# A graph kernel: where five pieces of work stand in the round of jobs, and which engine adds a bias

## The chip, the cores and the metric

The kernel runs on one core of a Trainium2 chip. A core has a matrix engine (TensorE, PE in the profile, with its weight loads shown as PEld), a vector engine (VectorE, DVE), an activation engine (ScalarE, ACT), a general engine (GpSimd, POOL) and a queue engine that only issues DMAs here (SyncE, SP). Matmuls write to PSUM, a small memory that VectorE and ScalarE read and write too. The metric is the device time of one execution in microseconds (us), lower is better.

## What is computed

There are 128 graphs with 128 nodes and 64 features each. Layer 0 normalises the features, takes the relu, and sums a message over all pairs of neighbours; layer 1 normalises again and multiplies with the weighted adjacency.

```python
h = max(layernorm(x), 0)
mask = adj > 0
A = h @ W1[:64] + h @ W1[64:] + b1          # per node j
C = h @ W1[64:]                             # per node k
hm[j] = sum over k of mask[j, k] * relu(A[j] - C[k])     # 192 hidden units
x = x + hm @ W2 + (number of neighbours of j) * b2
h = max(layernorm(x), 0)
x = x + (adj @ h) @ W.T
```

(Written here with the difference in the message multiplied out, as the kernel does it.) About one pair in eight is an edge, so the kernel doesn't compute all pairs: it gives every node j a fixed number of slots for its neighbours and gathers the neighbours' rows by matmuls with one-hot matrices.

## The kernel before, in words

**Groups.** The graphs are done in 32 groups of four (`G = 4`, `NG = 32`). A group's work has three parts: what is prepared in the round of the group ahead, the main jobs, and what is finished in the round of the group behind. In a node's neighbour list the 128 nodes k are cut into four quarters of 32 (`Q`, `QN`), and each node has six slots (`D`) in each quarter. The few neighbours beyond are handled by `edge_x`, `edge_sum` and `edge_sum1`, with the one-hot matrices `R`, `RT` and `S2`.

**Preparation** (table `AHEAD`, for group g + 1 in the round of group g):

- `pre_adj` transposes adj on TensorE (`pt`), copies it (`adjT`) and makes the mask (`maskT`, on VectorE; two buffers, so it waits until `edge_sum` of the group before last has read its own). It also starts the norm's statistics (`sta`, `mva`).
- `pre_norm` and `pre_hT` make the normalised features `h` and their transpose `hT`.
- `pre_rank` counts with one matmul (`pq`) which slot each neighbour takes; ScalarE copies the ranks to `qs`, VectorE marks the overflow (`ov`).
- `pre_slots`, in three pieces, compares the ranks with the slot numbers on VectorE and makes the one-hot matrix `S`. After the last piece twelve DMAs on SyncE's queue copy it into `S3`, in which the quarters stand three times below each other.
- `pre_count` (`pd`) counts neighbours and makes the small per-node factors `dn`, `ns`, `half`, `nb`.
- `pre_proj`, for r = 0 and r = 1, is the projection, of two graphs each: four fp32 matmul passes give C, A and the output row (`pp`, in one of the three large PSUM tiles `g`), and two bf16 matmuls add the biases to the columns from H on (`oneb` times `biasp`, a split of the fp32 bias into three bf16 parts in three rows). ScalarE copies the result to bf16 (`ca`, first part), makes `z` and `e` from it, VectorE subtracts the copy from the fp32 value (`rest`), ScalarE rounds that (second part), GpSimd the remainder (third part). So three bf16 parts stand for the fp32 value.
- `pre_stack`: twelve DMAs on SyncE's queue put the parts of `ca` into `k3`, by part and quarter.
- `pre_edge_a` to `pre_edge_d` and `pre_place` make the one-hot matrices of the overflowing edges.

**Jobs.** A round has 24 jobs (`Job`, times t = 0 to 23, list `ORDER`). A job fills one of three PSUM tiles `g`, each two banks, by matmuls of `k3` with `S3` and with an identity (`id3`), and drains it. A job of kind 0 has the first 128 hidden units of one graph; VectorE drains it with one reduction (`hm`). A job of kind 1 has the last 64 units of two graphs, one on each half of the columns; ScalarE takes the relu (`T`) and GpSimd sums. In a round four jobs of kind 0 are followed by two of kind 1, four times over, so t = 4, 5, 10, 11, 16, 17, 22, 23 are of kind 1. The jobs at t = 0 and 1 need the last of the twelve `k3` copies.

**Finishing** (table `BEHIND`, for group g − 1): `slot_sum` adds two halves on GpSimd; `edge_sum` (24 matmuls `pe`) and `edge_sum1` (ten) correct the sums and VectorE makes `u0` (128 units) and `u1` (64 units of two graphs); `post0` multiplies by W2 (`py`; `w2bd` takes `u1` over all columns, `w2h` takes `u0` on one half of the columns for each pair); `post1` transposes back (`pty`), adds `e` and computes the second norm's statistics; `post2` makes the second `h`; `post3` multiplies by the adjacency (`pga`, on halves of the columns); `post4` by W, adds, and stores.

**Order.** All matmuls run in the order in which the program writes them (`mm` and `tp` call `keep_in_program_order`): per t first the job's matmuls, then the pieces of `OWN`, `BEHIND` and `AHEAD` of that t. On the other engines and on SyncE's queue the written order is kept in the start only (`Engine.held`). In the rounds the framework's planner orders each queue when the program is built: of the instructions it believes to be ready it takes the one written first. That order is then fixed. The last group has its own list (`ORDERL`), and its finishing pieces run alone at the end.

Of the kernel before, what the change touches and what calls it, by code (L numbers as in the profile page):

```python
# [8 lines left out]
F32 = mybir.dt.float32  # L9
BF16 = mybir.dt.bfloat16  # L10
I32 = mybir.dt.int32
AF = mybir.ActivationFunctionType
ALU = mybir.AluOpType
# [137 lines left out]
def kernel(  # L151
# [28 lines left out]
    def mm(*args, **kw):  # L180
        return tc.keep_in_program_order(nc.tensor.matmul(*args, **kw))  # L181
# [21 lines left out]
    vec, act, pool, sp = (Engine(e) for e in (nc.vector, nc.scalar, nc.gpsimd, nc.sync))  # L203

    B, N, F = x.shape
    H = W1.shape[1]
    O = W2.shape[1]
    P = 128
# [19 lines left out]
    with ExitStack() as main:  # L228
        const = main.enter_context(tc.tile_pool(name="const", bufs=1))
        loads = main.enter_context(tc.tile_pool(name="loads", bufs=2))  # L230
        grp = main.enter_context(tc.tile_pool(name="grp", bufs=2))
        one = main.enter_context(tc.tile_pool(name="one", bufs=1))
# [4 lines left out]
        def gtile(name):  # L237
            return ps_g.tile([P, 2, 512], F32, tag="g", name=name)
# [10 lines left out]
        w2bd = const.tile([P, 2, O], F32, tag="w2bd", name="w2bd")  # L249
# [3 lines left out]
        ident = const.tile([P, P], F32, tag="ident", name="ident")  # L253
        make_identity(nc, ident)

        id64 = const.tile([P, 4], F32, tag="id64", name="id64")
        vec.tensor_tensor(id64, ident[:, 0:4], ident[:, F : F + 4], ALU.add)
        ones = const.tile([P, P], F32, tag="ones", name="ones")
        pool.memset(ones, 1.0)
        oneb = const.tile([P, P], BF16, tag="oneb", name="oneb")  # L260
# [11 lines left out]
        for q in range(Q):  # L272
            s = slice(q * QN, (q + 1) * QN)
# [43 lines left out]
        bias = const.tile([P, H + O], F32, tag="bias", name="bias")  # L317
        wp = const.tile([P, 2 * H + O], F32, tag="wp", name="wp")
        wab = wp[:, H : 2 * H]
        biasp = const.tile([P, H + O], BF16, tag="biasp", name="biasp")  # L320

        def weight_loads():
            act.dma_start(w2a, W2[0:C0, :])
# [33 lines left out]
            return pc  # L357

        def weights_c(pc):
            left = bias  # L360
            for i in range(3):
                pt = one.tile([P, H + O], BF16, tag=f"bp{i}", name=f"bp{i}")
                vec.tensor_copy(pt, left)

                if i == 0:
                    vec.tensor_scalar(biasp, pt, id64[:, i : i + 1], None, ALU.mult)
                    vec.tensor_copy(wp[:, 2 * H : 2 * H + O], pc[:, 0:O])
                else:
                    vec.scalar_tensor_tensor(
                        biasp, pt, id64[:, i : i + 1], biasp, ALU.mult, ALU.add  # L370
                    )
                if i < 2:
                    nxt = one.tile([P, H + O], F32, tag=f"br{i}", name=f"br{i}")
                    vec.tensor_tensor(nxt, left, pt, ALU.subtract)
                    left = nxt

        def weights_d():
            pl = mtile("pl")
# [5 lines left out]
        def bc(t, n, axis):  # L384
            shape = list(t.shape)
            shape.insert(axis, n)
            return t.unsqueeze(axis).to_broadcast(shape)
# [150 lines left out]
        def pre_proj(g, r):  # L538

            d = groups[g]  # L540
            if r == 0:

                d["ca"] = grp.tile([P, 3, 2, G, H], BF16, tag="ca", name=f"ca{g}")

                d["z"] = grp.tile([P, G, C0], F32, tag="z", name=f"z{g}")
                d["z1"] = grp.tile([P, 2, 2, C1], F32, tag="z1", name=f"z1{g}")
                d["e"] = grp.tile([P, G, O], F32, tag="e", name=f"e{g}", bufs=3)
            pp = gtile(f"pp{g}_{r}")
            for p in range(2):
                s = slice(p * F, (p + 1) * F)  # L550
                mm(
                    pp[:, p, 0 : 2 * H + O], d["hT"][s, r], wp[s, :],
                    start=True, stop=False, skip_group_check=True,
                )
            for p in range(2):
                s = slice(p * F, (p + 1) * F)
                mm(
                    pp[:, p, H : 2 * H + O], oneb[s, :], biasp[s, :],
                    start=False, stop=True, skip_group_check=True,
                )  # L560
            x = pp[:, :, 0 : 2 * H].rearrange("n p (t u) -> n p t u", t=2)
            parts = [
                d["ca"][:, i].rearrange("n t (p r) u -> n r p t u", p=2)[:, r] for i in range(3)
            ]
            act.activation(parts[0], x, AF.Copy)
            rest = tmp.tile([P, 2, 2, H], F32, tag="rest", name=f"rest{g}_{r}")

            def zs():
                for p in range(2):
                    b = 2 * p + r  # L570
                    for to, us, f in (
                        (d["z"][:, b], slice(0, C0), AF.Abs),
                        (d["z1"][:, r, p], slice(C0, H), AF.Relu),
                    ):
                        act.activation(to, x[:, p, 1, us], f, scale=d["ns"][:, b : b + 1])


            def es():
                for p in range(2):
                    b = 2 * p + r  # L580
                    act.activation(
                        d["e"][:, b], pp[:, p, 2 * H : 2 * H + O], AF.Copy,
                        scale=d["dn"][:, 0, b : b + 1],
                    )

            def second():
                act.activation(parts[1], rest, AF.Copy)

            def third(engine):
                for t in range(2):  # L590
                    engine.tensor_tensor(
                        parts[2][:, :, t], rest[:, :, t], parts[1][:, :, t], ALU.subtract
                    )

            def add_x():
                pool.tensor_tensor(d["e"], d["e"], d["x"], ALU.add)

            if g == 0:
                vec.tensor_tensor(rest, x, parts[0], ALU.subtract)
                return zs, es, second, third, add_x  # L600
            zs()
            es()
            vec.tensor_tensor(rest, x, parts[0], ALU.subtract)
            second()
            third(pool)
            if r == 1:
                add_x()
# [143 lines left out]
        def post0(g):  # L751
            d = groups[g]
            py = mtile(f"py{g}")
            d["py"] = py
            for p in range(2):
                s = slice(p * O, (p + 1) * O)
                mm(
                    py[s, 0 : 2 * N], w2h,
                    d["u0"][:, 2 * p : 2 * p + 2].rearrange("h r j -> h (r j)"),
                    start=True, stop=False, skip_group_check=True,  # L760
                )
            w = w2bd.rearrange("h p o -> h (p o)")
            mm(
                py[:, 0 : 2 * N], w, d["u1"].rearrange("h r j -> h (r j)"),
                start=False, stop=True, skip_group_check=True,
            )
            d["ys"] = tmp.tile([P, 2, N], F32, tag="ys", name=f"ys{g}", bufs=1)
            act.activation(
                d["ys"].rearrange("p r j -> p (r j)"), py[:, 0 : 2 * N], AF.Copy
            )  # L770
# [47 lines left out]
        class Job:  # L818
# [70 lines left out]

        AHEAD = {  # L890
            0: (pre_adj,),
            2: (pre_norm, pre_hT,),
            3: (pre_rank, lambda g: pre_slots(g, 0, 2),),
            4: (lambda g: pre_slots(g, 2, 4),),
            5: (pre_count,),
            6: (lambda g: pre_slots(g, 4, D),),
            7: (lambda g: pre_proj(g, 0),),
            9: (pre_edge_a,),
            12: (lambda g: pre_proj(g, 1), pre_stack,),
            19: (pre_edge_b,),  # L900
            20: (pre_place,),
# [7 lines left out]
        BEHIND = {  # L909
            0: (slot_sum,),  # L910
            1: (edge_sum,),
            4: (edge_sum1,),
            8: (post0,),
            10: (post1,),
            15: (post2,),
            16: (post3,),
            19: (post4,),
        }

# [33 lines left out]
        pc = weights_b()  # L953
# [80 lines left out]
```

## Time and profile before

| | us |
|---|---|
| median of three executions | 994.23 (993.23 to 1002.85) |
| the profiled execution | 1005.13 |
| its span, first to last instruction | 1003.4 |
| TensorE, VectorE, ScalarE, GpSimd busy | 947.9, 801.2, 706.3, 767.5 |
| SyncE waiting for a VectorE result before the `S` copies, in total | 256.3 in 29 times |
| one `S` copy, issue to landing, median | 4.0 |
| one `k` copy, issue to landing, median | 2.2 |

The page's busy time of TensorE counts matmuls that overlap in its pipeline and stretches in which one waits inside, so a high share does not say that it works at its best rate. A few of the costliest groups of instructions, as line, engine, operation, output<-inputs, shapes and count | busy us, mean ns of one | idle time before them and what ended it:

```profile
L198 DVE TENSOR_REDUCE hm<-g 128x64 f32<-128x768 f32 x512 | 473.4, 950 | 117.0 <-PE g L181 113.2
L181 PE MATMUL pp<-wp,hT 64*128 64x448 f32 x256 | 68.5, 613 | 0.0
L198 ACT ACTIVATE ca<-pp 128x768 bf16<-128x768 f32 x64 | 51.4, 804 | 63.7 <-PE pp L181 63.7
L198 DVE TENSOR_TENSOR rest<-pp,ca 128x768 f32<-128x768 f32 x64 | 60.7, 949 | 3.0 <-ACT ca L198 2.8
```

The line numbers are those of helpers: L181 and L184 are `mm` and `tp`, L198 is `Engine`, which passes on every call to the other engines. So instructions are told apart by the tiles that they write and read. Times in the timelines are the start from the span's beginning and the duration. "SPq" is SyncE's queue.

### The profile page before, as it was taken

The page shows a single profiled execution, that of the slowest core. Times are in us where ns is not written, and L with a number is a line of the kernel's source. Part 1 is how long each engine was busy: PE and PEld are TensorE (multiplying, and loading weights), DVE is VectorE, ACT ScalarE, POOL GpSimd, SP SyncE. Part 2 cuts the span into 40 slices and gives each one's busy share as a digit, 9 for nine tenths or more (in the row PEclk, how much of TensorE's full clock was granted, in tenths as well). Part 3 has the DMA queues.
Part 4 walks back from the last instruction along what each step waited for, and adds up shares of the span by engine and source line. Part 5 has one row for each costly group of instructions (what it writes and reads, how often), then busy time and mean ns, then how long its engine had stood idle before and what let it go on. Part 6 is the DMA issues. An engine that isn't in the chain of part 4 may idle for free.

```text
span 1003.4 us, 26630 instructions
## 1 busy us (share of the span) xinstructions
PE 947.9 (94%) x9994; PEld 695.8 (69%) x9994; DVE 801.2 (80%) x1769; ACT 706.3 (70%) x1732; POOL 767.5 (76%) x1134
## 2 busy tenths in 40 slices
PE   3899999999999999999999999999999999999996
PEld 2577776677776777777677767677767777777674
DVE  7677888877888878788887787887888887788863
ACT  5557876667877767787677785677787677787652
POOL 3287877787877878877788786778877788787783
PEclk9599999999999999999999999999999999999997
DMA  3626665556766555766555765555766655665520
GB/s 87 134 69 160 153 139 131 127 121 150 157 138 139 129 122 136 164 143 142 126 125 126 159 148 123 124 126 136 164 141 138 134 127 124 157 148 127 111 60 13
DMA packets 88293, 129.89 MB, mean 129 GB/s; under 512 B 47200, under 2 KB 63968, under 8 KB 88160
## 3 DMA queue, kind: packets, MB, share of 16 engines
q1 hardware_dynamic: 87584, 127.98, 56.4%
q8 instruction: 80, 1.31, 0.5%
q14 instruction: 53, 0.43, 0.1%
q10 hardware_dynamic: 576, 0.16, 0.1%
HBM read 13.01 MB, written 4.19 MB: 17 GB/s over the span
## 4 chain that ended last, share of the span: by engine, by line
PE 37%; DVE 23%; ACT 19%; DMA 7%; POOL 6%; issue 4%; SPq 3%; DVEq 0%; POOLq 0%; ACTq 0%
PE g L181 21%; DVE hm L198 7%; DVE S L198 7%; PE pe L181 7%; DMA k<-ca 6%; ACT ca L198 5%; ACT et L198 4%; POOL T L198 4%; SPq L198 3%; ACT h L198 3%; ACT T L198 3%; DVE u L198 3%; POOL ca L198 2%; ACT z L198 2%; PE px L181 2%
## 5 line engine op out<-in xcount | busy, mean ns | idle before, releaser
L198 POOL TENSOR_TENSOR T<-T 128x192 f32<-128x192 f32 (+2 forms) x768 | 545.7, 717 | 124.3 <-ACT T L198 84.4
L198 DVE TENSOR_REDUCE hm<-g 128x64 f32<-128x768 f32 x512 | 473.4, 950 | 117.0 <-PE g L181 113.2
L181 PEld LDWEIGHTS <-k 96*128 96x128 bf16 (+1 forms) x6144 | 412.8, 104 | 213.9 <-issue 87.0
L181 PE MATMUL g<-S,k 96*128 96x384 bf16 (+1 forms) x2048 | 392.5, 333 | 34.9 <-DMA k<-ca 18.5
L181 PE MATMUL g<-id,k 96*128 96x192 bf16 (+1 forms) x4096 | 383.9, 248 | 0.0
L198 ACT ACTIVATE T<-g 128x768 f32<-128x768 f32 x256 | 210.2, 823 | 51.7 <-PE g L181 45.7
L198 POOL TENSOR_TENSOR ca<-rest,ca 128x384 bf16<-128x384 f32 x126 | 113.9, 924 | 85.3 <-ACT ca L198 83.6
L198 ACT ACTIVATE ca<-pp 128x768 bf16<-128x768 f32 x64 | 51.4, 804 | 63.7 <-PE pp L181 63.7
L198 DVE TENSOR_TENSOR S<-qs,rks 128x1024 bf16<-128x1024 bf16 x93 | 86.8, 934 | 0.0
L198 ACT ACTIVATE hT<-ph 128x256 f32<-128x256 f32 x32 | 12.3, 384 | 89.4 <-PE ph L184 89.4
L181 PE MATMUL pe<-RT,X 128*64 128x128 f32 (+1 forms) x512 | 71.3, 282 | 0.0
L181 PE MATMUL pp<-wp,hT 64*128 64x448 f32 x256 | 68.5, 613 | 0.0
L198 ACT ACTIVATE z<-pp,ns 128x128 f32<-128x128 f32 (+1 forms) x256 | 66.0, 348 | 0.0
L198 DVE TENSOR_TENSOR rest<-pp,ca 128x768 f32<-128x768 f32 x64 | 60.7, 949 | 3.0 <-ACT ca L198 2.8
L198 ACT ACTIVATE ca<-rest 128x768 bf16<-128x768 f32 x64 | 55.2, 862 | 9.3 <-DVE rest L198 9.2
L181 PEld LDWEIGHTS pe<-RT,X 128*64 128x64 f32 (+1 forms) x512 | 53.4, 166 | 5.3 <-issue 5.3
L198 ACT ACTIVATE et<-et,half 128x128 f32<-128x128 f32 x128 | 56.8, 449 | 0.0
L181 PE MATMUL px<-ca,S 128*128 128x192 bf16 x384 | 52.7, 246 | 0.0
L181 PE MATMUL px<-ca,R 128*128 128x192 bf16 x384 | 52.6, 246 | 0.0
L198 ACT ACTIVATE h<-x,mrb,rsb 128x64 f32<-128x64 f32 x128 | 51.6, 479 | 0.8 <-DVE mrb L198 0.8
L181 PE MATMUL pe<-ident,z 128*128 128x128 f32 x192 | 49.9, 287 | 0.0
L198 ACT ACTIVATE h<-x,mra,rsa 128x64 f32<-128x64 f32 x128 | 48.7, 432 | 1.1 <-DVE mra L198 1.1
(128 smaller groups left out, 1203.9 us busy)
## 6 DMA issues: line engine op xcount, KB each, us to landing
S<-S SPq DMA_DIRECT2D x372, 192.0 KB, 4.0
k<-ca SPq DMA_DIRECT2D x384, 96.0 KB, 2.2
adj<-in_adj_dram SPq DMA_DIRECT2D x32, 256.0 KB, 3.1
x<-in_x_dram SPq DMA_DIRECT2D x32, 128.0 KB, 2.7
out_dram<-ot SPq DMA_DIRECT2D x32, 128.0 KB, 2.2
w<-in_L_gnn_W_dram SPq DMA_DIRECT2D x2, 96.0 KB, 4.4
bias<-in_L_gnn_b_dram ACTq DMA_DIRECT2D x1, 96.0 KB, 3.8
w2a<-in_L_gnn_W_dram ACTq DMA_DIRECT2D x1, 32.0 KB, 2.1
```

Source lines behind the costliest of these rows:

```text
L181: return tc.keep_in_program_order(nc.tensor.matmul(*args, **kw))
L198: ins = f(*args, **kw)
```

## The change

Three things change.

1. **The bias.** The two bias matmuls of each projection go, with `biasp` and what made it at the start (`id64` and the loop in `weights_c`). In their place VectorE adds the fp32 bias to columns H to 2H + O of both banks of the PSUM tile, in place, in one instruction of 128 x 512 elements. The copy `ca`, `z`, `e` and `rest` read the tile after that.
2. **The order inside `post0`.** The matmul with `w2bd`, on all columns, comes first, and the two with `w2h`, on a half of the columns each, come last.
3. **The tables.** `pre_rank` moves from t = 3 to 2, `pre_edge_a` from 9 to 8, `edge_sum1` from 4 to 3, `post0` from 8 to 9, `post1` from 10 to 13, `post2` from 15 to 14, `post3` from 16 to 17. So `edge_sum1` and `post0`, which end with matmuls on halves of the columns, stand right before two jobs of kind 1, and `post3` right behind two of them.

```diff
         def weights_c(pc):
-            left = bias
-            for i in range(3):
-                pt = one.tile([P, H + O], BF16, tag=f"bp{i}", name=f"bp{i}")
-                vec.tensor_copy(pt, left)
...
+            vec.tensor_copy(wp[:, 2 * H : 2 * H + O], pc[:, 0:O])
...
                 mm(
                     pp[:, p, 0 : 2 * H + O], d["hT"][s, r], wp[s, :],
-                    start=True, stop=False, skip_group_check=True,
-                )
-            for p in range(2):
-                s = slice(p * F, (p + 1) * F)
-                mm(
-                    pp[:, p, H : 2 * H + O], oneb[s, :], biasp[s, :],
-                    start=False, stop=True, skip_group_check=True,
-                )
+                    start=True, stop=True, skip_group_check=True,
+                )
+            biased = pp[:, :, H : 2 * H + O]
+            vec.tensor_tensor(biased, biased, bc(bias, 2, 1), ALU.add)
...
             d["py"] = py
-            for p in range(2):
-                s = slice(p * O, (p + 1) * O)
-                mm(
-                    py[s, 0 : 2 * N], w2h,
-                    d["u0"][:, 2 * p : 2 * p + 2].rearrange("h r j -> h (r j)"),
-                    start=True, stop=False, skip_group_check=True,
-                )
             w = w2bd.rearrange("h p o -> h (p o)")
             mm(
                 py[:, 0 : 2 * N], w, d["u1"].rearrange("h r j -> h (r j)"),
-                start=False, stop=True, skip_group_check=True,
-            )
+                start=True, stop=False, skip_group_check=True,
+            )
+            for p in range(2):
+                s = slice(p * O, (p + 1) * O)
+                mm(
+                    py[s, 0 : 2 * N], w2h,
+                    d["u0"][:, 2 * p : 2 * p + 2].rearrange("h r j -> h (r j)"),
+                    start=False, stop=True, skip_group_check=True,
+                )
...
         AHEAD = {
             0: (pre_adj,),
-            2: (pre_norm, pre_hT,),
-            3: (pre_rank, lambda g: pre_slots(g, 0, 2),),
+            2: (pre_norm, pre_hT, pre_rank),
+            3: (lambda g: pre_slots(g, 0, 2),),
             4: (lambda g: pre_slots(g, 2, 4),),
             5: (pre_count,),
             6: (lambda g: pre_slots(g, 4, D),),
             7: (lambda g: pre_proj(g, 0),),
-            9: (pre_edge_a,),
+            8: (pre_edge_a,),
...
         BEHIND = {
             0: (slot_sum,),
             1: (edge_sum,),
-            4: (edge_sum1,),
-            8: (post0,),
-            10: (post1,),
-            15: (post2,),
-            16: (post3,),
+            3: (edge_sum1,),
+            9: (post0,),
+            13: (post1,),
+            14: (post2,),
+            17: (post3,),
             19: (post4,),
         }
```

More of the change, by code (lines that the diff above doesn't have):

```diff
@@ L254 @@
         make_identity(nc, ident)
-        id64 = const.tile([P, 4], F32, tag="id64", name="id64")
-        vec.tensor_tensor(id64, ident[:, 0:4], ident[:, F : F + 4], ALU.add)
         ones = const.tile([P, P], F32, tag="ones", name="ones")
@@ L319 @@
         wab = wp[:, H : 2 * H]
-        biasp = const.tile([P, H + O], BF16, tag="biasp", name="biasp")
         def weight_loads():
@@ L359, in weights_c @@
         def weights_c(pc):
-            left = bias
-            for i in range(3):
-                pt = one.tile([P, H + O], BF16, tag=f"bp{i}", name=f"bp{i}")
-                vec.tensor_copy(pt, left)
[L365 to L370, printed above, removed]
-                    )
[L372 to L375, printed above, removed]
+            vec.tensor_copy(wp[:, 2 * H : 2 * H + O], pc[:, 0:O])
         def weights_d():
@@ L754, in post0 @@
             d["py"] = py
+            w = w2bd.rearrange("h p o -> h (p o)")
+            mm(
+                py[:, 0 : 2 * N], w, d["u1"].rearrange("h r j -> h (r j)"),
+                start=True, stop=False, skip_group_check=True,
+            )
             for p in range(2):
@@ L759, in post0 @@
                     d["u0"][:, 2 * p : 2 * p + 2].rearrange("h r j -> h (r j)"),
-                    start=True, stop=False, skip_group_check=True,
+                    start=False, stop=True, skip_group_check=True,
                 )
-            w = w2bd.rearrange("h p o -> h (p o)")
-            mm(
-                py[:, 0 : 2 * N], w, d["u1"].rearrange("h r j -> h (r j)"),
-                start=False, stop=True, skip_group_check=True,
-            )
             d["ys"] = tmp.tile([P, 2, N], F32, tag="ys", name=f"ys{g}", bufs=1)
```

## The prediction

> **What bounds the kernel now.** I read the busy shares first, then the waits, then one steady group on the SyncE, VectorE, ScalarE and TensorE timelines. The shares would say TensorE:
>
> ```profile
> PE 947.9 (94%) x9994; PEld 695.8 (69%) x9994; DVE 801.2 (80%) x1769; ACT 706.3 (70%) x1732; POOL 767.5 (76%) x1134
> ```
>
> But the waits say that TensorE is stopped by the DMAs that bring `k3` in:
>
> ```profile
> PE g L181 <- DMA k<-ca: 18.5, 22, 7.2
> PEld L181 <- DMA k<-ca: 15.5, 29, 2.4
> ```
>
> (Total, times, longest.) The 7.2 is the start; after it TensorE or its weight loads, which can wait for the same copy, are stopped in nearly every group. So something else closes the loop. Follow one group. VectorE first:
>
> ```profile
> 335.53 0.78 DVE L198 TENSOR_SCALAR maskT<-adjT 128x512 bf16<-128x512 f32 x1 [1.14 <-PE pe L181]
> 336.83 1.81 DVE L198 TENSOR_REDUCE hm<-g 128x64 f32<-128x768 f32 x2
> 340.84 1.00 DVE L198 TENSOR_TENSOR S<-qs,rks 128x1024 bf16<-128x1024 bf16 x1
> 341.97 2.81 DVE L198 TENSOR_REDUCE hm<-g 128x64 f32<-128x768 f32 x3
> 344.70 0.95 DVE L198 TENSOR_TENSOR rest<-pp,ca 128x768 f32<-128x768 f32 x1
> ```
>
> SyncE's queue and then TensorE:
>
> ```profile
> 341.87 10.16 SPq L198 DMA_DIRECT2D S<-S  x12
> 352.12 9.30 SPq L198 DMA_DIRECT2D k<-ca  x12
> ```
> ```profile
> 361.14 0.32 PE L181 MATMUL g<-S,k 96*128 96x384 bf16 x1
> 361.79 0.34 PE L181 MATMUL g<-S,k 96*128 96x384 bf16 x1 [0.32 <-DMA k<-ca]
> 362.73 0.68 PE L181 MATMUL g<-S,k 96*128 96x384 bf16 x2
> ```
>
> The loop: `maskT` starts at 335.53; VectorE works without a gap until the last `S` piece is done at 341.84 (6.3 us); SyncE issues twelve `S` copies (to 352.03) and twelve `k` copies without a gap (to 361.42, 19.6 us together); the last `k` lands 2.2 us after its issue, near 363.0; TensorE then finishes the job at t = 1 and the 24 matmuls of `edge_sum` (2.03 us), and the next `maskT` starts at 365.87. That is 30.3 us. TensorE's spare time is read from the same rows: a job takes 0.66 us (355.33 to 355.99); the job at t = 0 took from 361.14 to 362.29, the one at t = 1 from 362.73 to 363.58, so 0.49 + 0.19 = 0.7 us of waiting. In the chain, `edge_sum` starts at 95.46 and at 963.06, 29 groups apart: 29.9 us a group. A group is as long as this loop, and a change moves the time if it moves a term of the loop, or uses up the slack of what must be ready beside it. The slacks: TensorE's 0.7 us; and the second part of `ca`, which the fifth `k` copy needs.
>
> **The change, part by part, per group.**
>
> *Bias matmuls away (2 pairs).* The second pair starts at 349.15, the next job at 349.41: at most 0.26 us a pair. The least is its 256 columns at the rate of the id matmuls (four of 192 columns in 0.33): 0.11. TensorE saves 0.2 to 0.5.
>
> *Moved matmuls.* A job's four id matmuls take 0.33 us; where a piece with other rows or columns follows, a gap opens: 343.29 + 0.33 = 343.62, and `py` starts at 343.71. Such gaps are 0.09 to 0.16 each. `edge_sum1`, `post0` and `post1` now stand so that about five fewer occur: 0.5 us. [...] Together TensorE gets 0.7 to 1.0 us shorter, inside a slack, so by itself worth 0.
>
> *`pre_rank` from 3 to 2, `edge_sum1` from 4 to 3.* Between `maskT` and the last `S` piece VectorE has no gap, and the same instructions must still be done before it (two `hm`, `u` twice, `ov`, three `S`). Earlier ranks change their order, not their sum: 0. It would be one `hm` (0.87) either way, if the planner put a reduction behind or ahead of the last `S`; I keep both for the range.
>
> *The added VectorE instruction.* 128x512 fp32, read from PSUM and written there. No row writes PSUM from VectorE; with a PSUM source, 256 columns take 0.41, 512 take 0.676 (`u<-hs,pe`), 768 take 0.949 (`rest`). I take 0.68, between 0.41 and 0.95. Two a group: 1.4 us on an engine that had 2.4 idle behind t = 15 and none between 335.5 and 346.
>
> *What it puts in line.* The first copy `ca` of r = 0 ran at once, in ScalarE's idle time, while VectorE was late:
>
> ```profile
> 342.45 0.81 ACT L198 ACTIVATE ca<-pp 128x768 bf16<-128x768 f32 x1 [1.87 <-PE pp L181]
> 344.06 0.55 ACT L198 ACTIVATE e<-pp,dn 128x64 f32<-128x64 f32 x2
> 345.68 0.84 ACT L198 ACTIVATE ca<-rest 128x768 bf16<-128x768 f32 x1 [0.26 <-DVE rest L198]
> 349.61 0.80 ACT L198 ACTIVATE ca<-pp 128x768 bf16<-128x768 f32 x1
> 353.33 0.89 ACT L198 ACTIVATE ca<-rest 128x768 bf16<-128x768 f32 x1
> ```
>
> Now it waits for the add, and the add waits behind the reductions of t = 6 and 7, which are written before it and are ready: 341.97 + 2 × 0.87 + 0.68 = 344.4. So `ca` starts 2.0 us later. Queued behind it on ScalarE: `z`, `e`, the second copy, `ys`, `et`, and the copies of t = 10 and 11; ScalarE has no longer gap from 345.7 to 354. `rest` starts after `e` ends (344.61, then 344.70), so the projection's PSUM tile, one of three, is held to 347.6 and not 345.65. [...]
>
> *r = 1.* The tile for it is free between 348.4 (as before) and 349.6 (if only the reduction of t = 12 frees one); four matmuls take 0.85, so they end at 349.3 to 350.5 (before, with the bias pair, 349.4). The add goes behind that reduction: 349.6 to 350.6. From `ca` to the end of the second part is 4.6 us in the rows (349.61 to 354.22), with the add and a hand-over 5.3 less the 0.4 that ScalarE spent on other work: 354.5 to 355.5. The fifth `k` copy is due at 352.12 + 4 × 0.775 = 355.2. So this slack, 1.0 now, goes to between 0.7 and −0.3.
>
> *`post1` 10 to 13, `post2` 15 to 14, `post3` 16 to 17.* From `pty` (346.39) to the last `h` (353.49) is 7.1 us now; bare, the pieces sum to 3.9 (0.44 + 0.42 + 0.60 + 0.36 + 0.29 + 0.35 + 1.4). Behind `pty` TensorE now has four jobs (2.8) and two `px` (2.0) before `pga`: 4.7. So the wait at `pga` is 0 (bare) to 2.4 (with as much queueing as now); I take 0.3, near the bare sum because `post2` now stands directly behind. From the end of the projection to `pga` it is five jobs (3.4), `pty` 0.37 and the two `px`: 5.8. TensorE reaches t = 18 at 349.9 (middle) + 5.8 + 0.3 + 0.44 = 356.4, against 355.33 before: 1.1 late, its own savings already in it. Less the slack of 0.7: **+0.4 us a group**. Bounds: an early tile and no wait, 349.3 + 5.8 + 0.44 = 355.5, inside the slack: 0. A late tile and a wait of 1.0: 357.7, 1.7 over.
>
> *Once.* At the start eight short VectorE instructions (2.9 us) go; TensorE waits 2.07 there for `ov`, whose ranks come little earlier; two adds (1.4) come in. −1 to +0.5, taken as 0. At the end `py` starts with the later operand: +0.4, left out.
>
> Sum: 30 × 0.4 = +12 us on the profiled execution's 1005.13 us (span 1003.4), so 1017. That execution lies 10.9 above the median of 994.23; I put the same +12 on the median: **1006 us**.
>
> **Rivals.**
>
> *The slack swallows all of it* (994, from 986 to 1002). For it: 0.7 us of TensorE slack plus 0.7 to 1.0 saved, and SyncE's 19.6 us untouched. Against: ScalarE has no gap to take 2 us of shifted work.
>
> *Faster.* It needs a shorter loop, and the one term that can shrink is the 6.3 us before `S`: if the earlier `qs` lets the planner take the last `S` before one reduction, −0.87 × 30 = −26: 968; half that if it happens in part of the groups, 981. It decides at whether the last `S` is issued before the reduction of t = 3. Against: that reduction is written first and ready.
>
> *Slower by another place.* The last `S` starts at 340.84, just when the reduction of t = 6 gets ready. If the planner puts that first, +0.87 × 30 = +26: 1020, with the forecast's term 1032.
>
> *The add costs other than taken.* 0.41 to 0.95 each, twice, on the path: ±16 at most; inside the range.
>
> **How the numbers follow.** Forecast case 0.37, slack swallows 0.35, `S` later 0.13, faster 0.15. The range runs from 980 (half the groups gaining) to 1036 (both slower cases, and a little), leaving out some 0.15; the bound of 1.7 a group (1045) lies outside it, since it needs both extremes in every group. Over 1% is 10 us, about what a measurement of this kernel can tell from no change. Faster 0.15, within 1% 0.35, slower 0.50.
>
> **What would show it.** Right: ScalarE's first `ca` of a group waits for VectorE's `pp`, about 2 us later against the last `S`; TensorE waits for `h` at `pga` or for a free `g` tile near t = 12; its waits for `k` get smaller; SyncE's twelve and twelve take the same time. Wrong: the span from `maskT` to the last `S` differs from 6.3 us, or TensorE still waits 0.7 us or more for `k` in every group.

## The result, and the profile after

The changed kernel takes 1131.41 us (median of six executions, 1128.7 to 1135.12) against 996.29 for the kernel before beside it. The ratio is 1.135, with a 95% interval of 1.131 to 1.139. It is 135 us slower where the prediction had 12, and lies far outside its range. The profiled execution took 1130.92, its span is 1129.1.

The busy times of VectorE, ScalarE and GpSimd are within 6% of those before and TensorE's is 4% longer; as the span is an eighth longer, all their shares are lower:

```profile
PE 989.8 (88%) x9866; PEld 725.4 (64%) x9866; DVE 847.3 (75%) x1824; ACT 707.0 (63%) x1732; POOL 758.4 (67%) x1134
```

What has changed is what TensorE waits for. The longest of its waits in the changed kernel (total, times, longest):

```profile
PE pga L181 <- ACT h L198: 40.3, 61, 2.7
PE pp L181 <- ACT T L198: 31.6, 30, 1.1
PE g L181 <- DVE hm L198: 16.6, 30, 0.8
PE g L181 <- DVE rest L198: 13.8, 30, 0.5
PE pq L181 <- DVE u L198: 10.5, 30, 1.1
PE g L181 <- DMA k<-ca: 8.3, 1, 8.3
```

Of the waits for `k` one is left, at the start. In every group there are now others: for `h` at `pga`, for a PSUM tile that `T` or `rest` still reads, and for `u` at `pq`. Here is one group, VectorE first (start, duration, engine and line, operation, in brackets the idle time before):

```profile
204.52 0.43 DVE L198 TENSOR_SCALAR maskT<-adjT 128x512 bf16<-128x512 f32 x1 [1.13 <-PE pe L181]
...
209.34 1.41 DVE L198 TENSOR_TENSOR S<-qs,rks 128x1024 bf16<-128x1024 bf16 x1
...
210.88 1.80 DVE L198 TENSOR_REDUCE hm<-g 128x64 f32<-128x768 f32 x2
212.61 0.68 DVE L198 TENSOR_TENSOR pp<-pp,bias 128x512 f32<-128x512 f32 x1
...
215.50 0.96 DVE L198 TENSOR_TENSOR rest<-pp,ca 128x768 f32<-128x768 f32 x1 [0.35 <-ACT e L198]
```

From `maskT` to the end of the last `S` piece (210.75) it is 6.23 us, as before. The add stands behind two reductions, as expected. Then ScalarE and SyncE's queue:

```profile
213.33 0.81 ACT L198 ACTIVATE ca<-pp 128x768 bf16<-128x768 f32 x1 [3.60 <-DVE pp L198]
...
215.32 1.31 ACT L198 ACTIVATE et<-iov,mid 128x128 f32<-128x128 f32 x4
216.50 0.86 ACT L198 ACTIVATE ca<-rest 128x768 bf16<-128x768 f32 x1
217.25 0.39 ACT L198 ACTIVATE ys<-py 128x256 f32<-128x256 f32 x1
217.51 1.52 ACT L198 ACTIVATE T<-g 128x768 f32<-128x768 f32 x2
...
226.88 1.42 ACT L198 ACTIVATE h<-x,mrb,rsb 128x64 f32<-128x64 f32 x4
```
```profile
210.78 9.94 SPq L198 DMA_DIRECT2D S<-S  x12
221.66 8.73 SPq L198 DMA_DIRECT2D k<-ca  x12
```

`ca` starts 2.58 us behind the last `S` piece (0.61 before). Behind it ScalarE has no gap up to 222.97; of these rows the two `T` copies, which free PSUM tiles, come last, behind four `et` of `pre_edge_a`. The four `h` that `pga` needs end at 228.30. SyncE's twelve and twelve take 9.9 and 8.7, no longer than before; between them stand 0.94 us, up to the end of the `ca` of r = 1 (221.64). TensorE in the same group:

```profile
216.51 0.48 PE L181 MATMUL g<-S,k 96*128 96x384 bf16 x2 [0.46 <-DVE rest L198]
218.38 1.02 PE L181 MATMUL pp<-wp,hT 64*128 64x448 f32 x4 [1.05 <-ACT T L198]
219.34 0.82 PE L181 MATMUL g<-S,k 96*128 96x384 bf16 x2
...
220.59 0.63 PE L184 MATMUL pty<-ident,ys 128*128 128x128 f32 x2
...
227.37 0.43 PE L181 MATMUL pga<-adjT,h 128*64 128x128 f32 x2 [0.64 <-ACT h L198]
228.03 0.76 PE L181 MATMUL pga<-adjT,h 128*64 128x128 f32 x6 [0.23 <-ACT h L198]
228.72 0.50 PE L181 MATMUL g<-S,k 96*128 96x384 bf16 x2
```

The job at t = 18 starts at 228.72, 17.9 us behind the first `S` copy's issue; before it was 13.5 (355.33 less 341.87). So it is 4.5 us late, where the prediction had 1.1. The four waits above sum to 2.4 of it (a fifth, 0.54 for `hm` at t = 8, the kernel before has too). Most of the rest is in no list of waits. It shows in the table of windows of the same group (stretch, its length, then busy time and count of PE, PEld, DVE, ACT and POOL, then the granted clock, DMA share, GB/s):

```profile
212.49:215.90 3.41, 3.39 (x41) 2.39 (x38) 3.06 (x7) 2.57 (x9) 1.54 (x4) 1.00 0.99 204
215.90:219.31 3.41, 1.90 (x14) 0.85 (x10) 1.52 (x2) 3.41 (x9) 1.88 (x3) 1.00 0.98 223
219.31:222.73 3.42, 3.42 (x19) 2.58 (x18) 2.18 (x4) 3.39 (x12) 3.18 (x5) 0.51 1.01 208
222.73:226.14 3.41, 3.41 (x45) 2.97 (x45) 3.41 (x13) 2.37 (x8) 2.54 (x5) 1.00 0.42 117
```

In the stretch with the waits for `rest` and `T`, TensorE is busy for 1.90 of 3.41 us. In the next 3.42 us the granted clock is 0.51, and 19 matmul records fill it, against 45 in the stretch behind it; the two matmuls that start at 219.34 take 0.82 us, the same two at 216.51 and 228.72 take 0.48 and 0.50. Between 110 and 960 us such half-clock stretches sum to 89 us in the changed kernel and to 3.4 in the kernel before.

### The profile page after: what moved, and what is told of

Read it like the earlier page. It is cut to its first block, busy times and chain, and to the rows that moved or that the text cites. A ratio compares the mean times of both kernels' runs of the same rounds, so it can differ in the third digit from the quotient of the medians.

```text
span 1129.1 us, 26551 instructions
## 1 busy us (share of the span) xinstructions
PE 989.8 (88%) x9866; PEld 725.4 (64%) x9866; DVE 847.3 (75%) x1824; ACT 707.0 (63%) x1732; POOL 758.4 (67%) x1134
## 4 chain that ended last, share of the span: by engine, by line
PE 44%; ACT 27%; DVE 20%; issue 5%; DMA 3%; POOL 1%; DVEq 0%; POOLq 0%; ACTq 0%
PE g L181 23%; DVE S L198 8%; PE pe L181 6%; ACT T L198 5%; ACT ca L198 5%; ACT et L198 4%; DVE hm L198 4%; ACT z L198 3%; DMA S<-S 3%; ACT h L198 3%; PE px L181 3%; PE pga L181 2%; PE pp L181 2%; DVE u L198 2%; DVE rest L198 2%
## 5 line engine op out<-in xcount | busy, mean ns | idle before, releaser
L198 POOL TENSOR_TENSOR T<-T 128x192 f32<-128x192 f32 (+2 forms) x768 | 534.0, 701 | 174.7 <-ACT T L198 133.7
L181 PEld LDWEIGHTS <-k 96*128 96x128 bf16 (+1 forms) x6144 | 437.9, 106 | 233.8 <-issue 121.3
L181 PE MATMUL g<-S,k 96*128 96x384 bf16 (+1 forms) x2048 | 401.1, 340 | 40.2 <-DVE hm L198 16.6
L181 PE MATMUL g<-id,k 96*128 96x192 bf16 (+1 forms) x4096 | 400.1, 253 | 0.0
L198 ACT ACTIVATE T<-g 128x768 f32<-128x768 f32 x256 | 199.9, 810 | 67.6 <-PE g L181 66.2
L198 DVE TENSOR_TENSOR pp<-pp,bias 128x512 f32<-128x512 f32 x64 | 44.2, 691 | 44.4 <-PE pp L181 37.2
L198 ACT ACTIVATE qj<-pj 128x512 bf16<-128x512 f32 x32 | 19.1, 597 | 92.3 <-PE pj L181 92.3
L181 PE MATMUL pga<-adjT,h 128*64 128x128 f32 x256 | 41.1, 324 | 40.3 <-ACT h L198 40.3
L198 POOL TENSOR_TENSOR hs<-hm 128x256 f32<-128x256 f32 x64 | 46.3, 724 | 42.2 <-DVE rsa L198 34.8
L181 PEld LDWEIGHTS pga<-adjT,h 128*64 128x64 f32 x256 | 20.4, 146 | 58.3 <-ACT h L198 54.6
```

Of the source, the lines that this page charges most:

```text
L198: ins = f(*args, **kw)
```

## The experiments

My theory on seeing this: TensorE, not the copy loop, now closes the group, and each of its new waits adds to the time. What had to be told apart is who makes the waits: the add alone, the moves alone, or the two only together; and, later, whether the clock is a cause of its own.

The table holds all runs. The length of a group is the mean distance of `pre_adj`'s transposes over 25 steady groups. The waits are TensorE's matmul waits between 110 and 960 us, brought to one group. The half-clock time is brought to one group in the same way. "Rest" is the group less its waits and less half of its half-clock time, which I take as the most that a halved clock can cost (an estimate: above, two matmuls took 0.82 us at half clock and 0.48 and 0.50 at full).

| kernel | us | ratio to before (95%) | group | waits | half clock | rest |
|---|---|---|---|---|---|---|
| before | 996 to 1001 | 1 | 29.9 | 0.85 | 0.1 | 29.0 |
| third `maskT` buffer | 983.0 | 0.978 to 0.990 | 29.2 | 0.2 | 0 | 29.0 |
| the same, `pre_rank` at 2 | 994.5 | 0.991 to 0.995 | 29.7 | 0.9 | 0.1 | 28.8 |
| add at r = 0 | 1007.8 | 1.005 to 1.012 | 30.2 | 1.3 | 0 | 28.9 |
| add at r = 1 | 1017.7 | 1.013 to 1.020 | 30.3 | 1.1 | 0 | 29.2 |
| add at both | 1037.0 | 1.030 to 1.043 | 31.1 | 1.9 | 0 | 29.1 |
| add twice at both | 1206.0 | 1.199 to 1.212 | 36.8 | 4.1 | 7.2 | 29.1 |
| moves alone | 1059.1 | 1.053 to 1.065 | 31.8 | 2.4 | 1.0 | 28.9 |
| moves, late `post3` | 1009.2 | 1.006 to 1.012 | 30.1 | 1.05 | 0 | 29.1 |
| after | 1131.4 | 1.131 to 1.139 | 34.2 | 3.6 | 3.6 | 28.8 |
| after, `post1` to `post3` at old places | 1127.3 | 1.122 to 1.135 | 34.1 | 3.5 | 4.9 | 28.1 |
| after, late `pre_edge_a` | 1124.3 | 1.120 to 1.128 | 34.0 | 3.35 | 3.3 | 29.0 |
| after, late `post3` | 1077.0 | 1.073 to 1.080 | 32.4 | 3.0 | 1.7 | 28.5 |
| after, late `post3`, late `pre_edge_a` | 1063.3 | 1.060 to 1.067 | 32.0 | 2.6 | 0 | 29.4 |
| after, useless matmuls at t = 12 | 1141.6 | 1.139 to 1.151 | 34.3 | 3.0 | 2.9 | 29.9 |
| after, the same at t = 12 and 17 | 1095.0 | 1.092 to 1.102 | 33.0 | 2.4 | 0 | 30.6 |
| before, the same at t = 12 and 17 | 1064.2 | 1.060 to 1.071 | 32.0 | 1.4 | 0 | 30.6 |

The rest lies between 28.1 and 29.4 us in every row but the last three, though the time runs from 983 to 1206. (In the last three 1.0, 1.6 and 1.6 us of useless matmuls are in it, so 28.9 to 29.0 without them.) So TensorE's own work is about 29 us a group, and what the change adds is waits of TensorE and half-clock time.

One caution for the whole table: nearly every edit also makes the planner write another order, so a run shows a piece together with the order that comes with it. Only the changed kernel and the two runs that add useless matmuls to it have the same order in their steady groups on both VectorE and ScalarE.

### One half of the change at a time

**The bias alone**, with the tables and `post0` as before.

```diff
-            for p in range(2): mm(pp[...], oneb[s, :], biasp[s, :], ...)
+            vec.tensor_tensor(biased, biased, bc(bias, 2, 1), ALU.add)
```

> The kernel before with the bias added by VectorE in place, and nothing moved: tables and the order in post0 as before. Theory A (the add is the cause: it stands behind two reductions, ScalarE's copy, the PSUM tile and TensorE wait behind it): most of the 135 us is here, 1060 to 1110 us, with ScalarE waiting some 3.5 us per group for VectorE's pp. Theory B (the moves are the cause: pre_edge_a in front of the T copies, and post3 too near to post1): 1000 to 1020 us, about the 12 us that were forecast for the add.

Measured: 1036.96, +37 on the kernel before. Between the two theories.

**The moves alone**, with the bias by matmuls.

```diff
-            8: (post0,),    10: (post1,),  15: (post2,),  16: (post3,),
+            9: (post0,),    13: (post1,),  14: (post2,),  17: (post3,),
```

(And `pre_rank`, `pre_edge_a`, `edge_sum1` and the order inside `post0`, as in the change.)

> The kernel before with the moves and the new order in post0, but the bias added by the two matmuls as before. Theory A: 985 to 1000 us, as the saved gaps between matmuls are hidden behind the k copies. Theory B: 1060 to 1110 us, with TensorE waiting 1 us or more per group for h at pga.

Measured: 1059.10, +59: just below the range of theory B, with the wait that it named. Table and order, which the prediction had at nothing or at 0.4 us a group, cost more than the add. Its waits:

```profile
PE pga L181 <- ACT h L198: 51.1, 61, 2.7
PE g L181 <- DVE hm L198: 14.4, 31, 0.7
PE pq L181 <- DVE u L198: 10.2, 30, 1.1
```

37 and 59 sum to 96, and both together cost 131 to 135. The parts are not independent.

### What bounded the kernel before

**A third buffer for `maskT`**, all else as before (two of the start's bias tiles share one, to make room).

```diff
-            d["maskT"] = grp.tile([P, G, N], BF16, tag="maskT", name=f"maskT{g}")
+            d["maskT"] = grp.tile([P, G, N], BF16, tag="maskT", name=f"maskT{g}", bufs=3)
```

> The kernel before with a third buffer for maskT, so that it need not wait for edge_sum (1.1 us per group in the profile of before); to make room two of the bias parts of the start share a buffer. If the kernel before is bound by the loop from maskT over the S and k copies to the next maskT, as the prediction said: the last S is done 0.7 us or more earlier and the time falls to 970 to 987 us, until TensorE's own work is the bound. If TensorE's work alone is the bound already: 992 to 998 us.

Measured: 983.01. That is where the prediction's loop says it should be: `maskT` no longer waits for `edge_sum`, the copies start earlier, and TensorE is left with its own 29 us. It is faster than both kernels.

**The same with `pre_rank` at 2 and `edge_sum1` at 3.**

```diff
-            2: (pre_norm, pre_hT,),
-            3: (pre_rank, lambda g: pre_slots(g, 0, 2),),
+            2: (pre_norm, pre_hT, pre_rank),
+            3: (lambda g: pre_slots(g, 0, 2),),
...
-            4: (edge_sum1,),
+            3: (edge_sum1,),
```

> before_mask3 with pre_rank at 2 and edge_sum1 at 3, the two moves that put no piece nearer to one that waits for it; the bias stays with the matmuls. If TensorE's work is the bound once the loop over the copies is shorter: the gaps between matmuls saved at edge_sum1 (0.2 to 0.3 us per group) show, 974 to 981 us. If the loop is still the bound: 980 to 986 us.

Measured: 994.50, ratio 0.991 to 0.995 against the kernel before; a miss, since it gives back 11 of the 17 us. From `maskT` to the end of the last `S` piece it now takes 8.0 us in the median of 25 groups (7.0 in the run above), and the waits for `k` are back (18.8 us; 10.9 above). So this move, priced at nothing, has a price where the loop is short.

### The spacing of the finishing pieces

**The changed kernel with `post1` to `post3` at their old places.**

```diff
-            13: (post1,),  14: (post2,),  17: (post3,),
+            10: (post1,),  15: (post2,),  16: (post3,),
```

> The changed kernel with post1, post2 and post3 back at 10, 15 and 16. If the wait for h at pga (40.3 us on TensorE, 1.3 us per group) is a loss by itself: 1075 to 1095 us. If it only follows from the late projection and comes back elsewhere: 1110 to 1131 us.

Measured: 1127.34, nearly nothing, as the second theory had it. The wait for `h` went, and another came, as `post1` now stands directly behind `post0` at 9:

```profile
PE pty L184 <- ACT ys L198: 73.6, 31, 2.4
```

**`post3` and `post4` two jobs later**, once without the add and once with it.

```diff
-            17: (post3,),  19: (post4,),
+            19: (post3,),  21: (post4,),
```

> moves_only with post3 at 19 in place of 17 and post4 at 21 in place of 19, so that two more jobs stand between post1 and post3. Theory 1 (the moves cost by the wait for h at pga, 51 us on TensorE in moves_only, because post1 at 13 and post3 at 17 leave too little time): the wait goes below 10 us and the time falls by 40 to 60, to 1000 to 1020 us. Theory 2 (ScalarE is late as a whole, and the wait only shows it): the wait moves to another piece, 1045 to 1060 us.

> The changed kernel with post3 at 19 and post4 at 21. Theory 1: the wait for h (40.3 us) goes, 1080 to 1095 us. Theory 2: 1115 to 1135 us.

Measured: 1009.24 and 1076.95, so 50 and 54 us less; theory 1 in both, the second a little below its range. The wait for `h` fell from 40.3 to 2.7 with the add, and without it from 51.1 to this:

```profile
PE pga L181 <- ACT h L198: 8.5, 29, 2.7
```

So of the 59 us of the moves 50 are one thing: `post3` too close behind `post2` (`post4` moved along with it). On top of the moves with a late `post3` the add costs 68 us, on top of the kernel before 37. What is left with the add is the second wait:

```profile
PE pp L181 <- ACT T L198: 31.6, 30, 1.1
PE g L181 <- DVE hm L198: 24.9, 46, 0.8
PE pq L181 <- DVE u L198: 19.4, 30, 0.9
PE g L181 <- DVE rest L198: 14.0, 30, 0.5
```

**`pre_edge_a` from 8 to 13**, so that its `et` no longer stand in front of the `T` copies. First alone:

```diff
-            8: (pre_edge_a,),
+            13: (pre_edge_a,),
```

> The changed kernel with pre_edge_a at 13 in place of 8, so that the four et instructions no longer stand ahead of the T copies of t = 10 and 11 on ScalarE. If that place is a cause (TensorE waits 31.6 us for T before the projection of r = 1): that wait goes below 8 us, and with what follows from it the time falls by 30 to 60, to 1070 to 1100 us. If the add alone makes those copies late: within 12 us of 1131.

Measured: 1124.27. The time is that of the second theory, but not its reason: the wait of `pp` for `T` went, as the first had said, and the time stayed because `pga` now waits 45.8 instead of 40.3, jobs wait 18.3 for `T`, and `px` waits 13.6 for `x`. TensorE comes to `pga` earlier and waits there. Then together with the late `post3`:

> The changed kernel with two of its moves undone together: post3 at 19 and post4 at 21 (which alone took 1077 us), and pre_edge_a at 13 (which alone took 1124 us, with the wait for T gone and that for h come in its place). If the two waits are each other's cover, so that taking one away lets the other one show, then both together give more than their sum (54 and 7): below 1060, the kernel being then near the one with the add alone, 1030 to 1055. If the T wait costs little, 1065 to 1077.

Measured: 1063.34, 14 us less than with the late `post3` alone: a little above the first range (below 1060) and a little below the second. The two undone moves sum to 61 us by themselves and give 68 together. The half-clock time went from 44 to 0 us between 110 and 960; at half the time lost in it that alone is up to 22.

### The price of the add

**The add at r = 0 or r = 1 alone**, the other half keeping its bias matmuls.

```diff
+            if r == 0:      # in the other run: r == 1
+                vec.tensor_tensor(biased, biased, bc(bias, 2, 1), ALU.add)
+            else:
                 (the two bias matmuls)
```

> The kernel before with the bias added by VectorE for r = 0 alone; r = 1 keeps its bias matmuls. The add at both places, with nothing moved, took 1037 us, 37 to 41 more than the kernel before. Theory 1 (place: the add of r = 0 stands behind two ready reductions and pushes the whole ScalarE queue of the group's middle, that of r = 1 finds nothing in front of it): nearly all of it, +28 to +41, so 1025 to 1041, and the wait of pga for h grows as with both. Theory 2 (price: each add costs its own 0.69 us and a hand-over on whichever engine is late): half, +15 to +23, so 1012 to 1023. Theory 3 (the r = 1 add alone matters, since it delays the second part of ca that the k copies need): within 6 of the kernel before.

> The counterpart: the bias added by VectorE for r = 1 alone; r = 0 keeps its bias matmuls. Theory 1 (place, r = 0): 0 to +10 on the kernel before, so 994 to 1010. Theory 2 (price): +15 to +23, 1012 to 1023. Theory 3 (r = 1): +28 to +41, and SyncE's k copies wait for the second part of ca in most groups. If the two halves add up to clearly less than the +37 to +41 of both, the two adds are not independent.

Measured: 1007.76 and 1017.70, so +8 and +18, and +37 for both. The theory of the place, which is the prediction's, is refuted: at r = 0, where `ca` comes 2 us later, 8 us are lost and not 28 to 41. The 18 of r = 1 lie in the range of the theory of the price, the 8 of r = 0 in no range. At r = 1 the planner wrote a different order. In the kernel before ScalarE does four `h` ahead of the second part of `ca`; with the add it does three, and VectorE's `mrb`, which `h` needs, stands behind the add and two reductions. ScalarE before, then VectorE and ScalarE of the run with r = 1 alone:

```profile
351.58 0.81 ACT L198 ACTIVATE h<-x,mrb,rsb 128x64 f32<-128x64 f32 x2
...
352.67 0.82 ACT L198 ACTIVATE h<-x,mrb,rsb 128x64 f32<-128x64 f32 x2
353.33 0.89 ACT L198 ACTIVATE ca<-rest 128x768 bf16<-128x768 f32 x1
```
```profile
356.70 0.70 DVE L198 TENSOR_TENSOR pp<-pp,bias 128x512 f32<-128x512 f32 x1
...
357.53 1.82 DVE L198 TENSOR_REDUCE hm<-g 128x64 f32<-128x768 f32 x2
359.27 0.30 DVE L198 SCALAR_TENSOR_TENSOR mrb<-mvb,rsb 128x4 f32<-128x4 f32 x1
```
```profile
359.44 0.59 ACT L198 ACTIVATE X<-px 128x256 f32<-128x256 f32 x2
359.86 1.15 ACT L198 ACTIVATE h<-x,mrb,rsb 128x64 f32<-128x64 f32 x3
360.86 0.89 ACT L198 ACTIVATE ca<-rest 128x768 bf16<-128x768 f32 x1
```

So its cost appears neither at `ca` nor at the `k` copies, but at `pga`, 19.6 us in 31 waits. The two halves sum to 26 of the 37.

**A second add of zeros behind each.**

```diff
             vec.tensor_tensor(biased, biased, bc(bias, 2, 1), ALU.add)
+            vec.tensor_tensor(biased, biased, bc(zero, 2, 1), ALU.add)
```

> The kernel with the bias added by VectorE and nothing moved, with a second add of the same shape, of a tile of zeros, right behind each of the two. What does 64 further adds of 0.69 us, 44 us of VectorE, come to? If VectorE's work in front of the copies is on the path of each group, all of it: 1037 + 40 to 50 = 1077 to 1087. If what cost 37 us was only the order of the queues (each copy now waiting for VectorE at all), the further adds cost little: 1037 to 1050. In both cases the order of the instructions, with the second add behind the first, is otherwise that of the single add.

Measured: 1206.04. Both ranges missed: 44 us of VectorE cost 169. It is not the price of the added time alone, because the order is another than with the single add, against what was expected: in each group a reduction stands between an add and the second one behind it, and ScalarE's copies `T`, `X` and the second part of `ca` are in another order too. The table says how the time was lost: per group 2.1 us more waits (4.1 against 1.9) and 7.2 us at half clock, of which up to 3.6 are lost; 2.1 and 3.6 sum to the 5.7 by which the group grew. It is the kernel that shows the clock most plainly (granted clock in 40 slices of the span, in tenths):

```profile
PEclk8799898998888988889899899888898888999998
```

### Is it the clock?

If a stretch with little work on TensorE is what brings the half clock, useless work there must make the kernel faster. The two runs below repeat a job's first matmuls, each repeat overwriting the one before; in a steady group the order on ScalarE and VectorE stays the same to the instruction.

```diff
-                for i in range(2):
+                for i in [0, 1] * (1 + more):      # more: t = 12: 3 (first run); 12: 3 and 17: 2 (second)
```

> The changed kernel with useless work for TensorE: the job at t = 12, right ahead of the projection of r = 1 that waits 1.05 us for T, does its first two matmuls four times over (each repeat overwrites the one before), six matmuls of 384 columns or some 1.0 us a group more. The order on the other engines is the same. Theory A (a stretch of 3.4 us in which TensorE is busy for less than some 0.6 is followed by one at half the clock, and that costs up to half of it): the wait for T shrinks by what is added, the stretch is busy for 0.8 and no longer followed by a half clock, and the kernel gets faster by useless work: 1131 less 15 to 45, so 1086 to 1116. Theory B (the clock has nothing to do with these waits): 1131, if the wait hides the work, to 1161, if it doesn't.

> As the one above, and also the job at t = 17, right ahead of post3's pga that waits for h, does its first four matmuls three times over, some 0.65 us more: 1.6 us of useless matmuls a group in all, 49 us over the kernel. Theory A: the half-clock stretches in the steady part go from 89 us to nearly none, and 1131 less 30 to 55, so 1076 to 1101. Theory B: 1131 to 1180. What is hidden in neither theory, a wait for h shorter than the work, is in both ranges.

Measured: 1141.56 (1131.55 to 1145.05) and 1095.02 (1094.76 to 1095.78). The first is a miss for theory A and in the range of B: the wait for `T` was filled, but TensorE then waited 52.0 instead of 40.3 for `h`, and behind that wait 72 us of half clock were left. With both filled there is none. Between 110 and 960 us, the changed kernel, then the one with both filled:

```profile
110.00:960.00 850.00, 760.11 (x7671) 560.08 (x7670) 645.51 (x1392) 547.82 (x1350) 585.39 (x870) 0.95 0.53 121
```
```profile
110.00:960.00 850.00, 786.86 (x8296) 583.56 (x8295) 666.88 (x1441) 563.24 (x1397) 608.12 (x903) 1.00 0.55 125
```

The clock went from 0.95 to 1.00, and 49 us of useless matmuls made the kernel 36 us faster. Every group now takes 33.0 us, which is what the changed kernel's groups without a half-clock stretch take (three of the 25 steady ones, 32.95 each; the mean of all is 34.2). So the clock costs 1.2 us a group, some 36 us in all.

The control, the same useless matmuls in the kernel before:

> The kernel before with the same useless matmuls at t = 12 and 17, 1.6 us a group. There is no low stretch and no half clock to take away here. TensorE has 0.85 us of waiting a group, so by either theory 0.75 to 1.6 us a group are added: 1000 + 22 to 48 = 1022 to 1048. If it gets faster or stays the same, the useless matmuls do something other than to keep the clock up, and the two runs above say nothing on the clock.

Measured: 1064.19, +67, more than expected (22 to 48). It is not a clean control: here the planner wrote another order on VectorE and ScalarE. A `T` copy now stands behind the next group's first `h`, and a job waits for it (28.2 us in 29 waits). What it does show is that the useless matmuls didn't make a kernel faster that had nearly no half clock to take away (3.4 us between 110 and 960 us); how much of the 67 us is the new order stays open. The reading above rests on the run with both places filled, where the order is the same.

## Why the prediction was wrong

- **What bounds the kernel before**: right. The third `maskT` buffer showed it. But TensorE's own 29.0 us stand only 0.85 us behind that loop; the 0.7 read from one group was about right, and it was all the room that the change had.
- **Bias matmuls and moved matmuls, 0.7 to 1.0 us of TensorE saved**: not seen. The rest is 29.1 with the moves (late `post3`), 29.1 with the add and 29.0 before, so no run here shows a gain from having fewer of the gaps. Nor does one open ahead of every piece with other rows: in the kernel before, a job's four id matmuls on 96 rows start at 350.39, and `px`, on 128, at 350.72, the 0.33 us of the id matmuls later.
- **`pre_rank` and `edge_sum1`, the sum ahead of the last `S` unchanged**: right for that sum, 6.23 against 6.3. As a price of 0 it was wrong: TensorE waits 10.5 us for `u` at `pq`, 30 times. The prediction asked what the move does to VectorE's sum and not what `pq` has to wait for.
- **The add at 0.68 us**: right, 0.691 on average over 64, with VectorE writing PSUM. **`ca` of r = 0 2.0 us later**: right, 1.97. What followed was named and priced too low. The prediction listed ScalarE's queue with the copies of t = 10 and 11 at its end, and the PSUM tile held 2 us longer; those copies and that tile are what TensorE waits for, 1.05 us for `T` and 0.46 for `rest` in each group. In the sum they stand only as a range for the tile of r = 1, of which it took the middle.
- **r = 1**: the projection ended at the late end of what was given (8.6 us behind the first `S` issue; 7.4 to 8.6 predicted, 8.0 taken). The fifth `k` copy, which was said to decide, decided nothing; the cost is at `pga`.
- **The failed step: "So the wait at `pga` is 0 (bare) to 2.4 (with as much queueing as now); I take 0.3, near the bare sum because `post2` now stands directly behind."** It is 1.2 us a group (30.2 us over the 25 groups between 110 and 960 us). In the three groups without a half-clock stretch it is 1.64. In the group shown it is 7.7 us from `pty` (220.59) to the last `h` (228.30), twice the bare 3.9 and more than the 7.1 of before. `post2` directly behind in the program didn't help, since on VectorE and ScalarE `rest`, reductions, `X` and `T` stand in between. The experiment with the late `post3` shows that this alone is worth 50 to 54 us.
- **Where the job at t = 18 lost its time, in the prediction's own terms**: it comes 3.4 us later than predicted (17.9 us behind the first `S` issue, 14.5 predicted). 0.5 of it is the projection (8.6 for 8.0). 1.6 is the way from there to `pga`, priced at 5.8 and measured at 7.4 (219.34 to 226.73): the same matmuls, nearly half of the way at half clock, which the sum didn't have. 1.25 is `pga` with its waits, priced at 0.3 + 0.44 and measured at 2.0 (226.73 to 228.72).
- **The sum, +0.4 a group**: 4.3 measured (34.2 less 29.9). In the three groups without a half-clock stretch it is 3.1, and there TensorE waits 4.0 us, 3.2 more than before: the waits are all of it. The half clock adds 1.2 in the mean. (Over all groups the waits grew by 2.75: `h` 1.2, `T` 1.05, `rest` 0.5, `u` 0.3, less 0.35 of the waits for `k`. That is less than 3.2 because in most groups with a half-clock stretch TensorE itself comes late to `pga` and waits 0.86 for `h` instead of 1.64.) The bound of 1.7 a group was given up because it "needs both extremes in every group"; but the planner's order on VectorE and ScalarE is the same in every steady group, so an extreme tends to come in all or in none. The 4.3 lie beyond that bound too.
- **The signs**: all that were named for being right came out (`ca` waits for `pp`, 2.0 us later; TensorE waits for `h` at `pga` and for a tile near t = 12; the waits for `k` are gone; SyncE's times and the 6.2 us are as before), and the time was wrong by 123 us. They named the places and no sizes.
- **The rivals**: none came about. TensorE became the bound, but by four waits, none of which had a rival of its own, and by the clock, which the prediction didn't look at.

Open: what the late `post3` kernel without the add still loses (8 us), why the two adds cost 11 us more together than one by one, and the 11 us of the earlier `pre_rank` in the kernel with three `maskT` buffers, were not followed further, nor how much of each run is the new order of the planner.

## What to carry to other kernels

Where one engine has less than a microsecond of room a group, price every wait that the change puts in front of it: for each instruction that the engine waits on, and for each buffer that it writes to, go through the queue of the engine that delivers or frees it, and don't stop at the first consumer. A piece that "stands directly behind" in the program does not do so on the engines whose order a planner fixes. And look at the clock by stretches beside the list of waits. Here waits of 0.46 and 1.05 us fell into one stretch of 3.41 us, in which TensorE was busy for 1.90, and in the next 3.42 us the granted clock was 0.51. So these waits cost more than their sum (by the run with both places filled the half clock adds 1.2 us a group), and the list of waits doesn't say so.

## What the hardware showed that was not expected

In the changed kernel the granted clock halves after short lulls. In the profiles of the kernel before and of the changed one it goes from 1.0 to 0.5 and back only at whole steps of 3.41 us. In the changed one, between 100 us and 35 us before the end, 25 such windows at half clock follow a window in which the matmuls were busy for 0.52 to 0.59 of the time (four more follow a halved window); the windows that stay at full clock follow 0.59 or more. With the late `post3` it is 0.55 against 0.69 or more, with the useless matmuls at both places the lowest is 0.70 and no window is halved. (The shares are worked out from the matmul records of the traces, whose ends are modelled, and the share does not settle it in every kernel. In the run with `post1` to `post3` at their old places eight windows of 0.50 to 0.54 were not followed by a half clock, and there 21 halved windows follow a halved one that was busy for 0.82 or more; with the add twice two windows of 0.61 were followed by a half clock. So by this share alone a half clock can't be foretold, and what else it hangs on was not shown.) The longest single wait in the window shown was 1.05 us, and between 110 and 960 us no matmul of the changed kernel waited longer than 1.4.
